# Placing the last row's receptance and first division behind a block step in a fused RWKV attention and mixture-of-experts kernel

## The chip, the core and the metric

The kernel runs on one core of a Trainium2 chip. A core has a matrix engine (PE, with its weight loads PEld), a vector engine (DVE), an activation engine (ACT), a general engine (POOL, which also issues the indirect DMAs) and SP, which here issues nearly all other DMAs. Each engine takes its instructions strictly in the order in which the program has them and waits at semaphores for the others. The metric is the device time of one execution in microseconds, the median of several runs.

## What is computed

The input x has 16 rows (batch entries) of 512 tokens of 256 channels, in float32. The reference, cut to what matters:

```
h   = layernorm(x)
xx  = h shifted by a token: channels 0-63 from before, 64-127 from behind
k, v, r = (h*mix + xx*(1-mix)) @ W.T          # three mixes, three weights
out = (a + exp(u+k)*v) / (b + exp(u+k))        # a, b: running sums over tokens
      a = a*exp(w) + exp(k)*v ; b = b*exp(w) + exp(k)
x2  = x + layernorm((sigmoid(r) * out) @ Wo.T)
t   = layernorm(x2)                            # 8192 tokens
y   = sum over the best 2 of 8 experts: gate * ((silu(t@w1.T+b1) * (t@w3.T+b3)) @ w2.T + b2)
z   = shared expert on every token, hidden width 512
result = x2 + layernorm(y + z)
```

## The kernel before

**Attention rows.** The loop over the 16 rows (L917) makes each row in steps. `front(b)` gives: sums, squares and the first norm (ACT), the turn to channels on partitions (PE transposes, L284), the mixes (DVE), the keys and values `k0` and `k1` (two halves of the channels: matmuls pk and pv at L346, exp to ek at L364 on ACT, and the two running sums at L371 on DVE), the receptance `r` (L349 to L352: four matmuls pr at L346, which the trace shows as eight pieces, and two exps to er on ACT), then per half a division `d0`, `d1` (L374 to L379: u joined to the sum, times 1 + er, and a reciprocal of 128x512, all on DVE) and a finish `f0`, `f1` (L381 to L384, giving g). `back(b)` gives the output matmuls po (L406) with their statistics, the residual and second norm, the router (L457 to L515), and eight indirect scatters of token rows into `xbuf`, a buffer in DRAM sorted by expert (L520).

**Expert blocks.** Once enough tokens of an expert lie in `xbuf`, a block of 256 of them is run. Blocks go through a pipeline, `push` (L704): one block step handles several blocks at different stages. In the order of the program it scales and scatters the oldest (`block_store`: ACT L689, POOL L691), transposes a new one (`block_turn`: px on PE L648, copied to xgT on ACT L650), makes the output of another (`block_out`: pq on PE L678, ye on DVE L682), makes the hidden layer of a third (`block_hidden`: pa and pb on PE L662, sil on ACT L665, he on DVE L667), and asks for the data of a new one (`block_load`: token rows xg at L637, weights we at L640, both on SP's queue). There are five buffers for xg, so a load of xg waits until the scatter that reads the buffer's old row numbers has landed. [...]

**The order.** For PE, DVE, ACT and SP it is written out by hand: every step of a row has a number in `ROW` (L32), with exceptions per row in `ROWS` (L33); `at(begin(b) + when[n], step)` (L889, L922) collects all steps with their times, and `in_order` (L892) issues them sorted by that number. The numbers are no times on the chip, only an order. `begin(b)` is 10 per row (L912), so row 15, the last, begins at 150. Block steps lie between the steps of the rows (L933 to L941). Around row 15's keys the order is: row 14's po1, row 15's k0 and k1 (152.61 and 152.82), row 14's residual x2 and its statistics stc (152.91 and 152.92), row 15's r (153.2) and d0 (153.51), a block step (153.9), another block step (155.9), then row 15's f0, d1 and f1 (157.4 to 157.42).

ACT evaluates exp and silu from different tables, and a table load stands in its queue where the function changes.

After the rows the rest of the blocks run back to back, then the shared expert for the remaining rows beside the loads of `ybuf` and the last norm.

Of the kernel before, what the change touches and what calls it, by code (L numbers as in the profile page):

```python
# [29 lines left out]
PERIOD = 10.0  # L30
START = [0.0, 10.0, 20.0, 30.0, 40.0]
ROW = {'x': -7.6, 'sum': -5.31, 'sq': -4.3, 'xn': -1.7, 'pt': -0.59, 'mix': 0.8, 'r': 3.2, 'k0': 2.61, 'k1': 2.82, 'd0': 3.51, 'f0': 7.4, 'd1': 7.41, 'f1': 7.42, 'po0': 9.6, 'po1': 12.6, 'x2': 12.91, 'stc': 12.92, 'xr': 17.9, 'pu': 19.21, 'pg': 19.52, 'pc': 20.43, 'sel': 21.5, 'pl': 19.22}  # L32
ROWS = {1: {'x': -8.3, 'sum': -5.6, 'sq': -4.51, 'xn': -2.5, 'pt': -1.99, 'mix': 0.0, 'r': 6.0, 'd0': 6.01, 'f1': 9.8, 'po0': 11.4, 'po1': 12.4, 'x2': 14.11, 'stc': 14.21, 'xr': 18.1, 'pu': 19.91, 'pg': 20.33, 'pc': 20.84, 'sel': 20.85, 'pl': 20.22}, 3: {'xn': -0.1, 'pt': 0.01, 'mix': 1.3, 'f0': 7.0, 'd1': 7.01, 'f1': 8.3, 'po0': 11.39, 'po1': 11.4, 'x2': 11.41, 'stc': 11.42, 'xr': 16.0, 'pu': 17.61, 'sel': 21.2, 'pl': 17.92}, 0: {'x': -7.1, 'sum': -5.11, 'sq': -1.1, 'xn': -1.09, 'pt': -1.08, 'mix': -1.07, 'r': 6.6, 'k0': -0.29, 'k1': 0.12, 'd0': 6.61, 'f0': 6.62, 'd1': 6.63, 'f1': 7.6, 'po0': 12.59, 'x2': 12.71, 'stc': 12.72, 'xr': 17.6, 'pu': 19.31, 'pg': 20.32, 'pc': 21.83, 'sel': 21.84, 'pl': 19.32}, 2: {'sq': -3.51, 'xn': -3.5, 'd0': 3.71, 'f0': 5.9, 'd1': 5.91, 'f1': 7.2, 'po0': 10.6, 'po1': 11.6, 'x2': 11.91, 'stc': 12.52, 'xr': 16.6, 'pu': 16.91, 'pc': 20.23, 'sel': 21.2, 'pl': 16.92}}  # L33
CONST_AT = 8
WHOLE_AT = -3.8
X_PARTS = 2
# [28 lines left out]
def kernel(  # L65
# [851 lines left out]
    for b in range(B):  # L917
        when = dict(ROW, **ROWS.get(b, {}))
        if b > 1:
# [178 lines left out]
```

## Time and profile before

| what | value |
|---|---|
| median of 3 runs | 1077.15 us (1076.97 to 1079.2) |
| profiled execution | 1082.54 us, span 1080.8 us |
| PE busy | 1012.6 us (94%) |
| DVE busy | 769.2 us (71%) |
| POOL busy | 569.2 us (53%) |
| ACT busy | 541.5 us (50%) |
| granted PE clock, mean | 0.979 |
| the reciprocals of the divisions (L379) | 32 of 3353 ns on DVE |
| row 15's receptance on PE | 702.26 to 705.70 us |
| row 15's first reciprocal | 711.92 to 715.27 us |

Times in the trace are microseconds from the start of the span. A row of the timeline gives the start, the duration, the engine, the line, the operation, out<-in and how many instructions were merged into it; in brackets stands how long the engine had been idle and what released it. Durations of neighbours on one engine overlap a little, so the distance between two starts tells more than a duration. Buffer numbers are left out of names. In a row of windows come the stretch, its length, the busy time and the number of instructions of PE, PEld, DVE, ACT and POOL, then the granted PE clock (1.00 is full), the DMA engines' busy share and GB/s.

### The profile page before, as it was taken

To read this page: it belongs to the slowest core of one execution; us is meant where nothing else is said; L and a number is where in the kernel's file an instruction comes from. 1 tells how busy PE (TensorE), PEld (TensorE's weight loads), DVE (VectorE), ACT (ScalarE), POOL (GpSimd) and SP (SyncE) were. 2 spreads that over 40 slices of the span, in tenths; PEclk is the share of its full clock that TensorE was granted. 3 is DMA by queue.
4 is the path that set the end of the run, shared out by engine and by line. 5 is a ranking of instruction groups with operands and counts; after the bars stand their busy time and mean duration, and the time that the engine had idled before them with its cause. 6 is when DMAs were issued, how large, how long until landed. Compare 5 with 4: busy or idle time off the path is not lost.

```text
span 1080.8 us, 15095 instructions
## 1 busy us (share of the span) xinstructions
PE 1012.6 (94%) x4202; PEld 701.4 (65%) x4202; DVE 769.2 (71%) x1905; ACT 541.5 (50%) x1150; POOL 569.2 (53%) x858
## 2 busy tenths in 40 slices
PE   5769898999999999999999999989999999999996
PEld 2335454767777677866768676667667878556554
DVE  4897696887797888878888887866353222478864
ACT  3355463657557484755757566543423333333341
POOL 2336435174656547465654646554442222369885
PEclk9789999999999999999999999989999999999998
DMA  4011313436465554645556464543556766879943
GB/s 161 6 39 38 112 71 126 151 120 192 146 200 159 175 186 154 215 153 169 154 184 189 163 192 156 171 162 119 164 196 217 246 217 207 282 246 314 314 143 114
DMA packets 80900, 181.68 MB, mean 168 GB/s; under 512 B 9597, under 2 KB 45583, under 8 KB 80816
## 3 DMA queue, kind: packets, MB, share of 16 engines
q1 hardware_dynamic: 67360, 144.89, 42.0%
q0 software_dynamic: 12736, 34.77, 8.7%
q10 hardware_dynamic: 720, 1.06, 0.3%
q8 instruction: 33, 0.54, 0.2%
q14 instruction: 51, 0.42, 0.1%
HBM read 123.12 MB, written 58.47 MB: 168 GB/s over the span
## 4 chain that ended last, share of the span: by engine, by line
PE 67%; issue 5%; ACT 4%; DVE 3%; POOL 3%; DMA 2%; SPq 0%; DVEq 0%; POOLq 0%; ACTq 0%
PE pq L678 10%; PE pa L662 9%; PE pz L749 8%; PE hs_pa L734 8%; PE pb L662 8%; PE hs_pb L734 7%; PE po L406 4%; PE pv L346 3%; PE pk L346 3%; PE pr L346 3%; PE px L648 2%; POOL xbuf L520 1%; DVE he L667 1%; PE pt L284 1%; ACT xr L278 1%
## 5 line engine op out<-in xcount | busy, mean ns | idle before, releaser
L691 POOL DMA_INDIRECT ybuf<-ye,xg x135 | 137.5, 1019 | 235.2 <-ACT ye L689 176.1
L520 POOL DMA_INDIRECT xbuf<-xr,place x128 | 134.7, 1052 | 94.3 <-DVE rest L515 46.7
L678 PE MATMUL pq<-we,he 128*128 128x256 f32 x540 | 134.2, 391 | 12.6 <-DVE he L667 11.8
L662 PE MATMUL pa<-xgT,we 128*128 128x256 f32 (+1 forms) x568 | 130.0, 372 | 0.0
L667 DVE SCALAR_TENSOR_TENSOR he<-pb,we,sil 128x256 f32<-128x256 f32 (+1 forms) x142 | 60.0, 463 | 96.7 <-PE pb L662 59.6
L662 PE MATMUL pb<-xgT,we 128*128 128x256 f32 (+1 forms) x568 | 128.3, 369 | 0.0
L734 PE MATMUL hs_pa<-xT,ws1t 128*128 128x512 f32 x256 | 120.6, 593 | 0.0
L734 PE MATMUL hs_pb<-xT,ws3t 128*128 128x512 f32 x256 | 120.3, 592 | 0.0
L678 PEld LDWEIGHTS pq<-we,he 128*128 128x128 f32 x540 | 97.6, 193 | 31.2 <-DVE he L667 17.4
L665 ACT ACTIVATE sil<-pa,we 128x256 f32<-128x256 f32 (+1 forms) x142 | 58.0, 460 | 117.7 <-PE pa L662 77.9
L749 PE MATMUL pz<-ws2t,hs 128*128 128x256 f32 x512 | 115.8, 380 | 0.2 <-DVE hs L740 0.2
L662 PEld LDWEIGHTS pa<-xgT,we 128*128 128x128 f32 x568 | 106.1, 193 | 14.2
L662 PEld LDWEIGHTS pb<-xgT,we 128*128 128x128 f32 x568 | 104.1, 190 | 13.2
L749 PEld LDWEIGHTS pz<-ws2t,hs 128*128 128x128 f32 x512 | 96.7, 190 | 19.8 <-issue 5.7
L379 DVE RECIPROCAL sb<-sb 128x512 f32<-128x512 f32 x32 | 107.3, 3353 | 1.1
L734 PEld LDWEIGHTS hs_pb<-xT,ws3t 128*128 128x128 f32 x256 | 48.6, 190 | 61.2 <-issue 56.7
L740 DVE SCALAR_TENSOR_TENSOR hs<-hs_pb,colt,hs_s 128x512 f32<-128x512 f32 x64 | 46.5, 733 | 51.9 <-PE hs_pb L734 21.7
L734 PEld LDWEIGHTS hs_pa<-xT,ws1t 128*128 128x128 f32 x256 | 48.3, 190 | 43.7 <-issue 40.1
L278 ACT ACTIVATE acc<-acc,nb_d,rs_d 128x256 f32<-128x256 f32 x64 | 34.9, 593 | 81.1 <-POOL nb_d L273 80.9
L682 DVE TENSOR_TENSOR ye<-pq,we 128x512 f32<-128x512 f32 (+1 forms) x71 | 46.7, 658 | 36.1 <-PE pq L678 31.8
L364 ACT ACTIVATE ek<-pk 128x512 f32<-128x512 f32 x32 | 18.9, 597 | 102.3 <-PE pk L346 53.7
L406 PE MATMUL po<-wa,g 128*128 128x256 f32 x256 | 63.1, 391 | 5.0 <-DVE g L384 4.9
(187 smaller groups left out, 1868.7 us busy)
## 6 DMA issues: line engine op xcount, KB each, us to landing
we<-in_we SPq DMA_DIRECT2D x71, 898.0 KB
xg<-xbuf SPq DMA_DIRECT2D x64, 258.0 KB
in<-ybuf SPq DMA_DIRECT2D x32, 512.0 KB
x<-in_x SPq DMA_DIRECT2D x15, 512.0 KB
out<-acc SPq DMA_DIRECT2D x30, 256.0 KB
x2s<-x SPq DMA_DIRECT2D x14, 512.0 KB
inx<-x2s SPq DMA_DIRECT2D x19, 256.0 KB
zs<-z SPq DMA_DIRECT2D x9, 512.0 KB
```

The lines of the kernel that those rows point to most:

```text
L346: nc.tensor.matmul(p, w[:, c, o * P : (o + 1) * P], r, start=(c == 0), stop=(c == NC - 1))
L379: nc.vector.reciprocal(sb, sb)
L406: nc.tensor.matmul(p[:, i, :], g[:, c, t * P : (t + 1) * P], woT[:, c, :], start=(c == 0), stop=(c == NC - 1))
L520: i = nc.gpsimd.indirect_dma_start(out=xbuf[:, :], out_offset=bass.IndirectOffsetOnAxis(ap=place[:, t, k : k + 1], axis=0), in_=xr[k][:, t ...
L662: nc.tensor.matmul(p[:, f, :], w[:, k : k + P], xgT[:, c, :], start=(c == 0), stop=(c == NC - 1))
L665: nc.scalar.activation(s[:, f, :], pp[0][:, f, :], AF.Silu, bias=w[:, O_B1 + f : O_B1 + f + 1])
L667: nc.vector.scalar_tensor_tensor(h[:, f, :], pp[1][:, f, :], w[:, O_B3 + f : O_B3 + f + 1], s[:, f, :], ALU.add, ALU.mult)
L678: nc.tensor.matmul(p[:, t, :], h[:, f, t * P : (t + 1) * P], w[:, k : k + C], start=(f == 0), stop=(f == NF - 1))
L682: nc.vector.tensor_tensor(y, p, w[:, None, O_B2 : O_B2 + C].to_broadcast([P, n, C]), ALU.add)
L691: j = nc.gpsimd.indirect_dma_start(out=ybuf[:, :], out_offset=bass.IndirectOffsetOnAxis(ap=xg[:, t, R_TO : R_TO + 1].bitcast(U32), axis=0) ...
L734: nc.tensor.matmul(p, w[:, c, f * P : (f + 1) * P], xT[:, c, :], start=(c == 0), stop=(c == NC - 1))
L749: nc.tensor.matmul(p[:, i, :], h[f][:, t * P : (t + 1) * P], ws2t[:, f, :], start=(f == 0), stop=(f == NS - 1))
```

## The change

Row 15 gets an entry of its own in `ROWS`, which moves its receptance from 153.2 to 155.2 and its first division from 153.51 to 155.51. Both now stand behind the block step at 153.9 and ahead of the one at 155.9. No step is added or taken out, and all other numbers stay. The diff, with the long line cut and written over several:

```diff
 ROWS = {
...
     2: {'sq': -3.51, 'xn': -3.5, 'd0': 3.71, 'f0': 5.9,
...
-}
+    15: {'r': 5.2, 'd0': 5.51}}
```

What this does to each engine's order, by the built programs:

- PE: the four pr matmuls stand behind px, pq, pa and pb of one block step instead of ahead of them.
- ACT: the two er stand behind that step's ye, xgT and sil. Before, they followed ek without a change of table; now one table load stands ahead of er and another ahead of the next sil, so ACT has two table loads more.
- DVE: L377, L378 and the reciprocal L379 of the first half stand behind that step's ye and he.
- POOL and SP: the same instructions in the same order.

More of the change, by code (lines that the diff above doesn't have):

```diff
@@ L32 @@
 ROW = {'x': -7.6, 'sum': -5.31, 'sq': -4.3, 'xn': -1.7, 'pt': -0.59, 'mix': 0.8, 'r': 3.2, 'k0': 2.61, 'k1': 2.82, 'd0': 3.51, 'f0': 7.4, 'd1': 7.41, 'f1': 7.42, 'po0': 9.6, 'po1': 12.6, 'x2': 12.91, 'stc': 12.92, 'xr': 17.9, 'pu': 19.21, 'pg': 19.52, 'pc': 20.43, 'sel': 21.5, 'pl': 19.22}
-ROWS = {1: {'x': -8.3, 'sum': -5.6, 'sq': -4.51, 'xn': -2.5, 'pt': -1.99, 'mix': 0.0, 'r': 6.0, 'd0': 6.01, 'f1': 9.8, 'po0': 11.4, 'po1': 12.4, 'x2': 14.11, 'stc': 14.21, 'xr': 18.1, 'pu': 19.91, 'pg': 20.33, 'pc': 20.84, 'sel': 20.85, 'pl': 20.22}, 3: {'xn': -0.1, 'pt': 0.01, 'mix': 1.3, 'f0': 7.0, 'd1': 7.01, 'f1': 8.3, 'po0': 11.39, 'po1': 11.4, 'x2': 11.41, 'stc': 11.42, 'xr': 16.0, 'pu': 17.61, 'sel': 21.2, 'pl': 17.92}, 0: {'x': -7.1, 'sum': -5.11, 'sq': -1.1, 'xn': -1.09, 'pt': -1.08, 'mix': -1.07, 'r': 6.6, 'k0': -0.29, 'k1': 0.12, 'd0': 6.61, 'f0': 6.62, 'd1': 6.63, 'f1': 7.6, 'po0': 12.59, 'x2': 12.71, 'stc': 12.72, 'xr': 17.6, 'pu': 19.31, 'pg': 20.32, 'pc': 21.83, 'sel': 21.84, 'pl': 19.32}, 2: {'sq': -3.51, 'xn': -3.5, 'd0': 3.71, 'f0': 5.9, 'd1': 5.91, 'f1': 7.2, 'po0': 10.6, 'po1': 11.6, 'x2': 11.91, 'stc': 12.52, 'xr': 16.6, 'pu': 16.91, 'pc': 20.23, 'sel': 21.2, 'pl': 16.92}}
+ROWS = {1: {'x': -8.3, 'sum': -5.6, 'sq': -4.51, 'xn': -2.5, 'pt': -1.99, 'mix': 0.0, 'r': 6.0, 'd0': 6.01, 'f1': 9.8, 'po0': 11.4, 'po1': 12.4, 'x2': 14.11, 'stc': 14.21, 'xr': 18.1, 'pu': 19.91, 'pg': 20.33, 'pc': 20.84, 'sel': 20.85, 'pl': 20.22}, 3: {'xn': -0.1, 'pt': 0.01, 'mix': 1.3, 'f0': 7.0, 'd1': 7.01, 'f1': 8.3, 'po0': 11.39, 'po1': 11.4, 'x2': 11.41, 'stc': 11.42, 'xr': 16.0, 'pu': 17.61, 'sel': 21.2, 'pl': 17.92}, 0: {'x': -7.1, 'sum': -5.11, 'sq': -1.1, 'xn': -1.09, 'pt': -1.08, 'mix': -1.07, 'r': 6.6, 'k0': -0.29, 'k1': 0.12, 'd0': 6.61, 'f0': 6.62, 'd1': 6.63, 'f1': 7.6, 'po0': 12.59, 'x2': 12.71, 'stc': 12.72, 'xr': 17.6, 'pu': 19.31, 'pg': 20.32, 'pc': 21.83, 'sel': 21.84, 'pl': 19.32}, 2: {'sq': -3.51, 'xn': -3.5, 'd0': 3.71, 'f0': 5.9, 'd1': 5.91, 'f1': 7.2, 'po0': 10.6, 'po1': 11.6, 'x2': 11.91, 'stc': 12.52, 'xr': 16.6, 'pu': 16.91, 'pc': 20.23, 'sel': 21.2, 'pl': 16.92}, 15: {'r': 5.2, 'd0': 5.51}}
 CONST_AT = 8
```

## The prediction

> **What bounds the kernel now.** The page first: PE is busy 94% of the span and holds 67% of the chain that ended last, so time is lost where PE stands still or runs slowly. Then the timeline of the stretch in which row 15, the last row, makes its keys and its receptance. I name blocks by the program's numbers: block 42's pq starts at 706.13, block 43's pq at 716.26, block 44's pa at 719.83, block 45's pa at 727.08, and the px at 724.46 is block 46's.
>
> ```profile
> 705.70 0.60 PE L648 MATMUL px<-ident,xg 128*128 128x128 f32 x4
> 706.13 1.89 PE L678 MATMUL pq<-we,he 128*128 128x256 f32 x8
> 707.86 1.89 PE L662 MATMUL pa<-xgT,we 128*128 128x256 f32 x8
> 709.59 1.89 PE L662 MATMUL pb<-xgT,we 128*128 128x256 f32 x8
> 711.32 0.60 PE L648 MATMUL px<-ident,xg 128*128 128x128 f32 x4
> 716.26 3.78 PE L678 MATMUL pq<-we,he 128*128 128x256 f32 x8 [4.34 <-DVE he L667]
> 719.83 3.06 PE L662 MATMUL pa<-xgT,we 128*128 128x256 f32 x8
> 722.73 1.89 PE L662 MATMUL pb<-xgT,we 128*128 128x256 f32 x8
> ```
>
> PE stands 4.34 us for block 43's he. Then pq takes 3.78 and pa 3.06 instead of 1.89: from 716.26 to 722.73 are 6.47 us for 3.46 of work (706.13 to 709.59), so 3.0 us more go to a slow clock. Why he is late stands on DVE:
>
> ```profile
> 711.92 3.35 DVE L379 RECIPROCAL sb<-sb 128x512 f32<-128x512 f32 x1
> 715.19 0.63 DVE L682 TENSOR_TENSOR ye<-pq,we 128x512 f32<-128x512 f32 x1
> 715.74 0.86 DVE L667 SCALAR_TENSOR_TENSOR he<-pb,we,sil 128x256 f32<-128x256 f32 x2
> ```
>
> Row 15's first division (L377 at 710.36, L378 at 711.19, the reciprocal) is queued ahead of ye and he, though sil (711.12 to 711.96) and pb were ready. Third view, the windows: from 735 to 782 PE is busy 47.00 of 47.00 us. What PE gains before 735 is therefore kept at least to 782; after that I find only chains that start from PE's results (router, scatters, block loads), so I carry the gain to the end.
>
> **The change, part by part.** The order of the two programs says: on PE the four pr matmuls go behind px, pq, pa, pb of one block step; on ACT the two er go behind that step's ye, xgT and sil; on DVE L377, L378 and the reciprocal go behind its ye and he. POOL and SP issue the same DMAs in the same order. ACT gets two table loads more. Nothing is taken out.
>
> PE: pr held 3.44 us (702.26 to 705.70). px 0.43, pq 1.73, pa 1.73 and pb 1.73 now start at 702.26 instead, then pr. Their inputs are there: he42 was done at 698.34, the wait for xg was over long before (load issued at 687.00), and the PSUM buffers that they and pr take over are read by 703.77 and 706.7, ahead of need. Total unchanged: block 45's px is again at 711.32. Cost 0, gain 0 up to here.
>
> ACT: x at 705.64 as before; ye at 707.45 in er's place, then by the old spacing xgT 708.24, table load 708.87, sil 710.16 to 711.00; new table load to 712.28, er 712.29 to 713.38, ye 713.25, xgT 714.04, second new load 714.67, block 44's sil 715.96 to 716.80 (its pa ends at 715.22). A load is 1.28 us on the row:
>
> ```profile
> 709.20 0.61 ACT L650 COPY xgT<-px 128x512 f32<-128x512 f32 x1
> 709.83 1.28 ACT L665 ACT_TABLE_LOAD   x1
> 711.12 0.84 ACT L665 ACTIVATE sil<-pa,we 128x256 f32<-128x256 f32 x2
> ```
>
> [...]
>
> DVE: ye at 710.36, he 710.9 to 711.8. Its first half is done before 711.5, so block 43's pq starts right behind px, at 711.75. The 4.34 us wait is gone, with the 3.0 us of slow clock behind it. Then L377 711.8; L378 waits for er to 712.9 (behind it stand the reciprocal, ye and he of block 44); reciprocal 713.6 to 717.0; ye 717.0; he 717.5 to 718.4.
>
> What is late next: PE runs pq 711.75, pa 713.48, pb 715.21 to 716.95, and wants block 46's px. Its xg load does not come earlier, for it waits for the scatters of block 41's ye, which POOL issues behind row 14's second norm:
>
> ```profile
> 710.53 0.60 POOL L268 TENSOR_SCALAR rs_c<-mv_c 128x4 f32<-128x4 f32 x1 [1.29 <-DVE mv_c L254]
> ...
> 713.89 1.09 POOL L691 DMA_INDIRECT ybuf<-ye,xg  x1 [0.62 <-issue]
> 715.29 0.97 POOL L691 DMA_INDIRECT ybuf<-ye,xg  x1 [0.30 <-issue]
> 717.98 0.31 SPq L637 DMA_DIRECT2D xg<-xbuf  x1
> ```
>
> That DVE result (710.44) stands ahead of everything that moved. The load's last landing is recorded at 720.70. So PE has a **new gap, 716.95 to 720.70: 3.75 us**, behind it pq, pa and pb. Then px 720.75, pq 721.18 (he is 2.8 us early), block 45's pa 722.91 instead of 727.08: **4.2 us earlier if the clock stays up**. The first division has slack too: from L383 at 725.50 to the last g at 733.77 were 8.27 us; from 718.4 that ends at 726.7, and PE wants g at 734.33 - 4.2 = 730.1.
>
> The clock is the other half. Windows of 3.41 us, laid on the times at which PEclk changes:
>
> ```profile
> 25.87:29.28 3.41, 1.35 (x4) 0.28 (x2) 3.27 (x4) 1.92 (x6) 2.32 (x3) 1.00 0.00 0
> 29.28:32.69 3.41, 2.49 (x8) 1.48 (x8) 3.37 (x3) 2.63 (x5) 0.29 (x3) 0.50 0.00 0
> 176.05:179.47 3.42, 1.50 (x4) 0.38 (x2) 0.47 (x2) 0.00 (x0) 2.65 (x5) 1.00 0.23 84
> 182.88:186.30 3.42, 3.42 (x5) 1.35 (x4) 2.82 (x10) 3.38 (x5) 2.04 (x4) 0.50 0.90 275
> 715.36:718.77 3.41, 2.51 (x6) 2.06 (x7) 1.24 (x3) 1.38 (x3) 2.73 (x3) 0.50 0.32 115
> 718.77:722.19 3.42, 3.42 (x9) 2.70 (x9) 0.69 (x1) 0.00 (x0) 0.12 (x1) 0.50 0.80 193
> ```
>
> First column the window, then PE's busy us; PEclk is the third number from the end. A window with 1.35 busy us is followed by half speed, one with 1.50 is not; a wholly busy window ends it, one with 2.51 doesn't. So a wait of some 2.0 us inside one window halves the clock. 3.75 us against windows of 3.41 does that for nearly every position (both parts stay under 2.0 only in 0.27 us of 3.41): one slow window costs 3.41/2 = 1.7 us, two cost the 3.0 seen now.
>
> **Sum** against the profiled execution (1082.54 us, span 1080.8): -4.2 + 1.7 = **-2.5 us** with one slow window, so 1080.0. The median of the runs is 1077.15, 5.4 below the profiled one; the stretch is the same in it, but its slow-clock share lies between 1.3 and 3.0 by the position of the windows (an estimate from the rows above). I take the same 2.5 off: **1074.6**.
>
> **Rivals.**
> - No slow window: -4.2, 1073.0. With the windows where this profile has them the gap is cut at 718.77 into 1.82 and 1.93, just under the threshold. [...] 0.20.
> - Two slow windows, as now: -4.2 + 3.0 = -1.2, 1076.0, within what counts as the same. It happens when a window ends 2.0 to 3.2 us into the gap, 1.2 of 3.41, less what the runs' own slow windows hide. 0.22.
> - The change doesn't do what it says, he43 being late by another wait (sil behind x on ACT): 1077.15. The order shows no such wait. 0.05.
> - **Slower**: block 46's xg lands later. Block 43's scatters now go out at about 719 instead of 724.44, into the stretch where this load (717.98 to 720.70) and a weight load run, the DMA engines being 0.64 busy from 717 to 722. The next weight load (issued 722.40) took 6.7 us to its last landing. At that length xg lands at 724.7, PE stands 4.0 us longer and two windows are slow: -4.2 + 4.0 + 3.0 = +2.8, 1080.0. With two slow windows it decides from 1.2 us of delay on. Against it: xg is issued ahead of those scatters. 0.13.
> - Forecast: 0.40.
>
> Range: from the case without a slow window with 1 us beyond it for the stall at 804 to 807 (PE 1.22 of 3.41 busy), which may fall in a kinder window, to the case without effect and 1 us: 1072.0 to 1078.2; only the slower case is left out. About 0.2%, 2.2 us, is what a measurement of this kernel can tell from no change. Faster: forecast and no slow window, 0.60; the same: two windows and no effect, 0.27; slower 0.13.
>
> **What would show it.** In the timeline after: px, pq, pa, pb at 702.3, pr behind pb at about 707.9; pq of block 43 at 711.8 with no wait; L379 at about 713.6; two more ACT_TABLE_LOAD rows; block 46's px at 720.7 with a wait of 3.7 us that ends with a DMA; its xg load still issued at 718.0; half speed from about 719 or 722 for one window; po of row 15 at 730 to 732 instead of 734.33. It is wrong if he43 is not done by 712, if xg is issued at another time, or if PE's lead at 735 is gone before the end.

## The result and the profile after

| | changed kernel | before |
|---|---|---|
| median of the first runs | 1076.57 us (21 runs, 1072.49 to 1078.99) | 1078.26 us (21 runs, 1076.96 to 1080.09) |
| median of later runs (beside run 9 below) | 1079.47 us (12 runs, 1077.46 to 1081.64) | 1082.84 us (26 runs, 1079.36 to 1084.99) |
| ratio, first runs | 0.998 (95%: 0.9971 to 0.9989) | |
| ratio, later runs | 0.9967 (0.9955 to 0.998) | |
| profiled execution, span | 1076.41 us, 1074.7 us | 1082.54 us, 1080.8 us |

The kernel is faster by 1.2 to 3.1 us by the first runs and by 2.2 to 4.9 us by the later ones. The two first profiles differ by more, 6.1 us, so the first question is where these lie. Here the same rows of PE stand beside each other in both profiles; he43 is short for block 43's he, and a slow window is one of the windows of 3.41 us in which the granted clock was 0.50:

| row on PE | before | after | after is later by |
|---|---|---|---|
| end of row 15's keys and values | 702.26 | 703.98 | +1.72 |
| row 15's po | 734.33 | 731.70 | -2.63 |
| hs_pa ahead of the wait near 805 | 791.61 | 788.82 | -2.79 |
| the hs_pa behind it | 813.85 | 806.93 | -6.92 |
| px at 917.59 before | 917.59 | 911.46 | -6.13 |

The stretch that the change touches, from the end of row 15's keys and values to its po, gives 4.35 us (32.07 us long before, 27.72 after). The start is 1.7 us later in this execution, long before anything that moved. Another 4.13 us come from one block's pq near 805 (told with runs 5 to 7), and 0.8 us are given back at 911. The stretch itself, after, on PE:

```profile
713.47 1.89 PE L678 MATMUL pq<-we,he 128*128 128x256 f32 x8
715.20 1.89 PE L662 MATMUL pa<-xgT,we 128*128 128x256 f32 x8
716.92 1.89 PE L662 MATMUL pb<-xgT,we 128*128 128x256 f32 x8
722.26 0.63 PE L648 MATMUL px<-ident,xg 128*128 128x128 f32 x4 [3.45 <-DMA xg<-xbuf]
722.73 1.89 PE L678 MATMUL pq<-we,he 128*128 128x256 f32 x8
724.46 1.89 PE L662 MATMUL pa<-xgT,we 128*128 128x256 f32 x8
```

Block 43's pq (first row) has no wait and no row is stretched by a slow clock. In their place stands one wait, 3.45 us for block 46's tokens, which a DMA ends. On the page the line of pq shows it too: its idle time for he is 5.9 us where it was 11.8.

```profile
L678 PE MATMUL pq<-we,he 128*128 128x256 f32 x540 | 130.9, 384 | 5.9 <-DVE he L667 5.9
```

DVE, after: block 43's he now stands ahead of the first division.

```profile
712.54 0.87 DVE L667 SCALAR_TENSOR_TENSOR he<-pb,we,sil 128x256 f32<-128x256 f32 x2
713.32 0.74 DVE L377 SCALAR_TENSOR_TENSOR sb<-ek,eu,sb 128x512 f32<-128x512 f32 x1
714.50 0.69 DVE L378 SCALAR_TENSOR_TENSOR sb<-er,sb 128x512 f32<-128x512 f32 x1 [0.43 <-ACT er L352]
715.23 3.35 DVE L379 RECIPROCAL sb<-sb 128x512 f32<-128x512 f32 x1
```

POOL and SP's queue, after: the scatters (the first two are block 41's) stand behind row 14's norm, and the load of xg behind them.

```profile
712.09 0.19 POOL L268 TENSOR_SCALAR rs_c<-mv_c 128x4 f32<-128x4 f32 x1 [1.29 <-DVE mv_c L254]
712.37 1.04 POOL L269 TENSOR_TENSOR rs_c<-rs_c,half 128x4 f32<-128x4 f32 x1
...
715.05 1.11 POOL L691 DMA_INDIRECT ybuf<-ye,xg  x1 [0.62 <-ACT er L352]
716.47 0.97 POOL L691 DMA_INDIRECT ybuf<-ye,xg  x1 [0.30 <-ACT xgT L650]
```

```profile
719.08 0.38 SPq L637 DMA_DIRECT2D xg<-xbuf  x1
```

The windows of this profile's clock grid (the 3.41 us steps at which its granted clock changes) that cut the wait, with PE's busy us first and PEclk third from the end:

```profile
716.87:720.28 3.41, 1.94 (x9) 1.36 (x8) 3.41 (x5) 2.39 (x5) 2.50 (x3) 1.00 0.33 102
720.28:723.69 3.41, 1.43 (x9) 1.35 (x10) 3.31 (x5) 0.59 (x1) 2.89 (x6) 1.00 0.90 204
```

Both keep more than 1.35 busy us, and the clock stays at 1.00 from 187.8 us to the tail of the kernel. The grid cuts the wait into two parts, 1.47 and 1.98 us of idle time in their windows. In the first profile of before it was otherwise: the window ahead of the two slow ones had no work of PE at all.

```profile
711.95:715.36 3.41, 0.00 (x0) 0.00 (x0) 3.41 (x2) 0.01 (x1) 2.40 (x5) 1.00 0.00 0
```

### The profile page after: what moved, and what is told of

It is laid out like the page before. It is cut to its first block, busy times and chain, and to the rows that moved or that the text cites. A ratio compares the mean times of both kernels' runs of the same rounds, so it can differ in the third digit from the quotient of the medians.

```text
span 1074.7 us, 15097 instructions
## 1 busy us (share of the span) xinstructions
PE 1009.1 (94%) x4202; PEld 699.9 (65%) x4202; DVE 767.5 (71%) x1905; ACT 544.3 (51%) x1152; POOL 570.3 (53%) x858
## 4 chain that ended last, share of the span: by engine, by line
PE 56%; DVE 9%; ACT 6%; DMA 5%; POOL 5%; issue 4%; SPq 0%; DVEq 0%; ACTq 0%; POOLq 0%
PE pq L678 8%; PE pz L749 8%; PE pa L662 7%; PE hs_pb L734 7%; PE hs_pa L734 7%; PE pb L662 7%; PE po L406 3%; PE pv L346 2%; PE pk L346 2%; DMA x<-in_x 2%; POOL xbuf L520 2%; PE pr L346 2%; DVE he L667 2%; DMA xg<-xbuf 1%; PE px L648 1%
## 5 line engine op out<-in xcount | busy, mean ns | idle before, releaser
L678 PE MATMUL pq<-we,he 128*128 128x256 f32 x540 | 130.9, 384 | 5.9 <-DVE he L667 5.9
L379 DVE RECIPROCAL sb<-sb 128x512 f32<-128x512 f32 x32 | 107.3, 3353 | 1.1
L278 ACT ACTIVATE x<-po,nb_b,rs_b 128x256 f32<-128x256 f32 x64 | 30.9, 563 | 72.5 <-DVE sa L371 33.2
```

The costliest lines, as they stand in the source:

```text
L278: nc.scalar.activation(dst, src, AF.Identity, bias=nb[:, t : t + 1], scale=rs[:, t : t + 1])
L379: nc.vector.reciprocal(sb, sb)
L678: nc.tensor.matmul(p[:, t, :], h[:, f, t * P : (t + 1) * P], w[:, k : k + C], start=(f == 0), stop=(f == NF - 1))
```

## The experiments

Theory: he43 was late because the division stood ahead of it on DVE. With that gone, block 46's tokens set when PE goes on, and they hang on POOL's order and on the number of buffers, not on what was moved. The slow clock decides the size of the gain. Rivals: the receptance's move matters (as cover for the wait, or by its two table loads); what PE gains is lost again later; the gain comes from the place near 805.

Runs 1 to 4, 5 to 8 and 9 to 12 are three sets, each on a chip of its own with before beside it. Before's medians were 1078.05, 1080.93 and 1082.84 us, so I compare ratios across sets.

**1. The division alone.** Edit of the changed kernel:

```diff
-    15: {'r': 5.2, 'd0': 5.51}
+    15: {'d0': 5.51}
```

> Only the division is moved (d0 at 155.51); the receptance stays at 153.2, so ACT has no table load more. Theory: the gain comes from the division leaving DVE's queue ahead of block 43's he, and then block 46's token load sets when PE goes on, whatever lies ahead of it. pq of block 43 then waits at most 0.6 us, block 46's px starts 18.3 us behind the end of row 15's keys and values (722.26 - 703.98 in the changed kernel), within 0.5, and the time is that of the changed kernel within 1 us, 0.7 to 2.7 below before. Rival 1: the receptance is needed behind the block step to cover the wait for he; pq then waits 2 us or more and the time is within 0.7 us of before. Rival 2: the two added table loads cost something in the changed kernel; this one is then over 1 us below it.

1074.74 us against 1078.05, ratio 0.9963 (0.9949 to 0.9977). On PE:

```profile
712.33 1.99 PE L678 MATMUL pq<-we,he 128*128 128x256 f32 x8 [0.25 <-DVE he L667]
...
720.30 0.63 PE L648 MATMUL px<-ident,xg 128*128 128x128 f32 x4 [2.53 <-DMA xg<-xbuf]
```

Block 43's pq waits 0.25 us, and block 46's px starts 17.87 us behind the keys (702.43 to 720.30; 18.28 in the changed kernel), both within what the theory gave. So the receptance isn't needed as cover. The time came out 3.3 us below before, a little more than the 0.7 to 2.7 expected; run 12 asks whether the table loads have a part in that.

**2. Work in the new wait.** The first of the shared expert's last steps goes ahead of block 46's px:

```diff
-        at(begin(B - 1) + ROW["po0"] + (i + 0.5) * (ROW["sel"] - ROW["po0"]) / LAST_BESIDE, shared_step)
+        at(begin(B - 1) + 6.5 if i == 0 else begin(B - 1) + ROW["po0"] + (i + 0.5) * (ROW["sel"] - ROW["po0"]) / LAST_BESIDE, shared_step)
```

> The changed kernel with the first of the shared expert's last steps (sixteen pz matmuls on PE, 3.46 us by their rows) moved from 160.6 to 156.5, ahead of block 46's px. Theory: the wait of 3.45 us for block 46's tokens is real time of PE and the lead is kept to the end; with work in it the wait at that px is under 0.6 us, no half speed starts in this stage, and the time falls by 3.0 to 5.5 us below the changed kernel (3.4 for the wait, up to 2 for the slow clock that follows it in some runs). Rival: what PE gains here is lost again at later waits; then the time is within 1 us of the changed kernel although the wait is gone.

1072.02 us, ratio 0.9945 (0.9932 to 0.9958):

```profile
718.27 3.62 PE L749 MATMUL pz<-ws2t,hs 128*128 128x256 f32 x16
722.31 0.66 PE L648 MATMUL px<-ident,xg 128*128 128x128 f32 x4 [0.43 <-DMA xg<-xbuf]
```

Of the wait 0.43 us is left. By the ratios this is 0.22% (later runs of the changed kernel) to 0.35% (first runs) below the changed kernel, 2.4 to 3.8 us, where 3.0 us left the wait. The ratios come from different chips, and the interval overlaps a little with that of the later runs (0.9955 to 0.998). On the same chip run 1's kernel, with a like wait of 2.53 us, had 1074.74 us, 2.7 above this one. So most of what left the wait reaches the end, and that speaks against a later loss.

**3. Six buffers for xg, after the change.**

```diff
-        xg = wp.tile([P, 2, R_END], F32, tag="xg", name=f"xg{q}", bufs=4 + LEAD)[:, 0:n]
+        xg = wp.tile([P, 2, R_END], F32, tag="xg", name=f"xg{q}", bufs=5 + LEAD)[:, 0:n]
```

> The changed kernel with six buffers for xg instead of five; same instructions in the same order. Theory: block 46's load waits for the scatters of block 41, which read the buffer that it takes over; with one buffer more it waits for block 40's, long landed, and is issued over 4 us earlier than 719.08; the wait of 3.45 us at block 46's px is under 0.5 and the time is 3.0 to 5.5 us below the changed kernel. Rival: the load is held by the queue of SP or by the weights' buffers, is issued within 1 us of now, and the time stays within 1 us.

1070.06 us, ratio 0.9932 (0.9919 to 0.9945), the fastest of set 1 and 4.7 us below run 1. Block 46's load goes out 4.0 us behind the keys' end (701.31 here) instead of 15.1 (719.08 - 703.98):

```profile
705.34 0.38 SPq L637 DMA_DIRECT2D xg<-xbuf  x1
```

```profile
715.98 0.60 PE L648 MATMUL px<-ident,xg 128*128 128x128 f32 x4
716.90 1.99 PE L678 MATMUL pq<-we,he 128*128 128x256 f32 x8 [0.32 <-DVE he L667]
```

The px has no wait, the next pq 0.32 us. This shows the chain from block 41's scatter over the buffer and the load to px: with another buffer the wait is gone.

**4. Row 14's norm behind the block step.** Edit of the changed kernel: `14: {'stc': 14.0}` added to `ROWS`.

> The changed kernel with row 14's second-norm statistics (stc) moved from 152.92 to 154.0, behind the block step at 153.9. Theory: block 41's scatters stand on POOL behind that norm; ahead of it they go out 3 us earlier, block 46's load is asked for at about 716 instead of 719.08, the wait at its px falls from 3.45 to under 1 us, and the time is 2.0 to 4.5 us below the changed kernel. Rival: the norm is then late for row 14's pu, whose rows already wait 0.16 us for xr; a wait of 2 us or more appears there and the time stays within 1.5 us of the changed kernel.

1072.75 us, ratio 0.9955 (0.9942 to 0.9968). POOL, SP's queue, then PE:

```profile
709.02 1.09 POOL L691 DMA_INDIRECT ybuf<-ye,xg  x1 [0.18 <-issue]
710.42 0.98 POOL L691 DMA_INDIRECT ybuf<-ye,xg  x1 [0.30 <-ACT sil L665]
```

```profile
713.06 0.38 SPq L637 DMA_DIRECT2D xg<-xbuf  x1
```

```profile
716.70 0.60 PE L648 MATMUL px<-ident,xg 128*128 128x128 f32 x4
719.10 1.99 PE L678 MATMUL pq<-we,he 128*128 128x256 f32 x8 [1.80 <-DVE he L667]
```

Counted from the keys' end (702.03 here) scatters and load are 4.1 us earlier than in the changed kernel (load 11.0 instead of 15.1), a little more than the 3 expected, and the wait for tokens is gone. The rival's wait (pu for xr) doesn't appear. Another does: the next block's he (718.57) stands behind the moved reciprocal (714.76 to 718.11), the mechanism of before one block later and 1.80 us long. Row 14's statistics (L253 and L254, 711.07 to 713.28) now stand on DVE between the block step's he and that division, so counted from the keys' end the reciprocal starts 1.5 us later than in the changed kernel; there the wait for tokens covers he's lateness, and in run 3 only 0.32 us of it was left.

**5 to 7. Second and third profiles of both kernels** (no edit).

> The kernel before once more, for a second profile. Theory: its first profile (1082.54 us, 4.4 above the median of its runs) holds a stall of 4.1 us at 804 to 812 that most runs do not have; it is missing here and the time lies between 1077 and 1080. The wait for block 43's he is again 4.3 us, within 0.3, and behind it lie one or two windows of half speed. Rival: the stall belongs to the kernel before, is here again, and the change took it away; the gain of the profiles is then due to that place as much as to the moved division.

> The changed kernel once more, for a second profile. Theory: its runs lie further apart (1072.5 to 1079.0) than those of before (1077.0 to 1080.1) because the wait for block 46's tokens lies at the edge at which the clock halves; the wait is 2.5 to 4 us again, and here, unlike in the first profile, one window or two of half speed may begin between 716 and 724, with 1.7 to 3.4 us more from the end of row 15's keys and values to po than the 27.7 of the first profile (731.70 - 703.98). Rival: this stretch is 27.7 us, within 0.7, whatever the run's time, and the runs differ elsewhere.

> The same kernel a third time, as before: the stretch from the end of row 15's keys and values to po is 27.7 us without a window of half speed, 29 to 31 with one or two (theory), or 27.7 within 0.7 whatever the run's time (rival).

Times 1078.79, 1075.83 and 1077.0 us, before's median beside them 1080.93. Before, again:

```profile
715.69 3.59 PE L678 MATMUL pq<-we,he 128*128 128x256 f32 x8 [3.63 <-DVE he L667]
...
804.78 1.99 PE L678 MATMUL pq<-we,he 128*128 128x256 f32 x8 [2.07 <-DVE he L667]
```

The wait for he43 is 3.63 us, shorter than I gave it, with one slow window (715.55 to 718.96) in place of two. The second row refutes my theory of the place near 805: the wait of about 2.1 us is in this profile too. But the rival falls as well, for the changed kernel has it in its second and third profile (2.05 and 2.06 us). All eight profiles of sets 2 and 3 have it, whichever kernel, and none of the four of set 1, which are all of kernels with the division moved. Something else in the traces goes with it. Before's first profile and these eight hold 10,444 to 10,687 semaphore counts of the engines; the first profile of the changed kernel and those of set 1 hold 13,388 to 13,392. So the wait goes with where or how a profile was taken, and no pair of profiles shows that the change took it away. I therefore don't count it as gain that before's first profile had it, with a slow window behind it (4.13 us), and after's lacked it. Whether the timed runs have this wait is not shown.

The stretch of the changed kernel was 27.09 and 27.59 us, the wait 2.82 and 3.30 us, no window slow. Here the rival is right: the stretch hardly varies.

**8. Six buffers without the change.**

> The kernel before with six buffers for xg instead of five. Theory: before, block 46's tokens are not what PE waits for; he43 behind the reciprocal is. The wait of 4.3 us for he43 stays, with its slow clock, and the time is 0 to 2 us below before (the wait of 1.0 us at 917 may go). The sixth buffer is worth 5 us or more only after the change (1070.1 against 1076.6 there). Rival: the sixth buffer is worth its 6 us everywhere, by loads that come earlier throughout; then this kernel is 5 us or more below before.

1080.78 us against 1080.93, ratio 0.9996 (0.9977 to 1.0014): nothing that can be measured. The wait for he43 stands as before, and the rows behind it are slow:

```profile
716.85 3.78 PE L678 MATMUL pq<-we,he 128*128 128x256 f32 x8 [4.20 <-DVE he L667]
720.42 3.15 PE L662 MATMUL pa<-xgT,we 128*128 128x256 f32 x8
```

The sixth buffer is worth 0.35 to 0.48% after the change (0.9932 against 0.9967 and 0.998) and nothing measurable ahead of it. In kernels with the division alone it is 0.32% (0.9931 of run 12 against 0.9963 of run 1).

**9. The changed kernel, timed again, with a fourth profile** (no edit).

> The changed kernel itself, timed beside the next three. Theory: 1.5 to 4.5 us below before, 27 to 28 us from the end of row 15's keys and values to po where no window is slow, and up to 3.4 more where one or two are. Rival: it is within 1 us of before on this chip, and the gain of 1.7 to 2.2 us measured at first was chance.

1079.47 us against 1082.84, ratio 0.9967. The stretch is 27.10 us, the wait 2.73. But in this profile a slow window begins 0.3 us ahead of row 15's po:

```profile
725.78:729.19 3.41, 2.39 (x25) 1.12 (x23) 1.32 (x3) 2.44 (x6) 1.03 (x1) 1.00 0.78 242
729.19:732.61 3.42, 3.37 (x9) 2.74 (x10) 2.40 (x18) 1.39 (x3) 0.00 (x0) 0.50 0.58 215
```

```profile
729.51 3.42 PE L406 MATMUL po<-wa,g 128*128 128x256 f32 x8
```

The po takes 3.42 us instead of 1.90. Counted from the keys' end, this execution is 4.97 us ahead of before's first profile at the start of po and only 2.79 ahead at the hs_pa ahead of the wait near 805. The slow window took 1.5 us of that, and a wait of 0.54 us for he at 761, which before's first profile lacks, most of the rest. So in this profile part of the gain of the stretch is lost a few us behind it.

**10 and 11. Idle matmuls inside each wait.** Nothing reads them; they only keep PE busy. In the changed kernel six of them ahead of block 46's px, in before seven ahead of block 43's pq:

```diff
+    def warm(n): [nc.tensor.matmul(p, ident, ws2t[:, 0, :], start=True, stop=True) for p in ([bank([P, C], "warm")] if n else []) for _ in range(n)]
...
-        q, xg, n = i["q"], i["xg"], i["n"]
+        q, xg, n = i["q"], i["xg"], i["n"]; warm(6 if q == 46 else 0)
```

> The changed kernel with six idle matmuls (ident by ws2t, twelve pieces of 0.22 us, 2.6 us; nothing reads them) ahead of block 46's px, inside the wait for its tokens. PE then has too little idle time there for a slow window, and no work is saved. Theory: in the changed kernel's runs the wait is often followed by a slow window; this one is then 0.7 to 2 us below the changed kernel. Rival (all three profiles so far had no slow window there): the clock costs nothing there, and the times agree within 0.6 us.

> The kernel before with seven idle matmuls (3.0 us; nothing reads them) ahead of block 43's pq, inside the wait for he. The wait for he stays as long, only the slow clock behind it goes. Theory: one or two windows are slow there in every profile of before, worth 1.2 to 3.0 us; this kernel is 1.2 to 3.0 us below before, and the wait alone (4.3 us) remains. Rival: the clock costs under 0.7 us in most runs; then this one is within 0.7 us of before, and the change should have gained the whole of its 4.2 us less what the wait for tokens costs.

Changed kernel with them: 1080.69 us, ratio 0.9989 (0.9975 to 1.0003), against 0.9967 without. That is 1.2 us above the changed kernel, with intervals that overlap: not the gain of the theory, nor the 0.6 us of the rival. In the profile the tokens came late: px starts 19.16 us behind the keys' end, against 17.56 to 18.28 in the four profiles of the changed kernel, so that 1.65 us of wait followed the idle work. If the timed runs are like that, the lateness could hide a small gain; that no clock is lost in that wait rests on the four profiles.

```profile
715.81 2.75 PE L632 MATMUL warm<-ws2t,ident 128*128 128x256 f32 x12
720.22 0.66 PE L648 MATMUL px<-ident,xg 128*128 128x128 f32 x4 [1.65 <-DMA xg<-xbuf]
```

Before with them: 1078.16 us against 1082.84, ratio 0.9962 (0.9947 to 0.9976), 2.6 to 5.7 us faster though PE gets he43 no earlier (pq starts 14.22 us behind the keys' end, 14.00 in before's first profile):

```profile
712.50 3.19 PE L632 MATMUL warm<-ws2t,ident 128*128 128x256 f32 x14
717.23 1.99 PE L678 MATMUL pq<-we,he 128*128 128x256 f32 x8 [1.54 <-DVE he L667]
```

```profile
712.77:716.18 3.41, 2.92 (x14) 2.23 (x12) 3.38 (x3) 0.17 (x1) 2.48 (x4) 1.00 0.00 0
716.18:719.60 3.42, 2.37 (x11) 2.08 (x12) 1.73 (x5) 1.38 (x3) 2.66 (x3) 1.00 0.32 115
```

No window is slow here, and the pq takes 1.99 us instead of 3.78. I expected 1.2 to 3.0 us; the interval begins at 2.6, and what goes beyond the clock of this stretch is not explained. The median granted clock of all runs rose from 0.980 to 0.984. This edit, which shortens no wait, was worth as much on this chip as the whole change (0.9962 and 0.9967). The changed kernel's runs there had 0.984 as well, and its stretch is 2.3 us shorter in the profiles (27.10 against 29.37); that these 2.3 us of time reach the end does not show in the runs of this chip.

**12. The division alone, with six buffers.** Edits of runs 1 and 3 together.

> Only the division moved (receptance back at 153.2, no table load more) and six buffers for xg. With the wait for block 46's tokens gone, what the receptance's move and its two table loads cost or gain can be seen. Theory: nothing; the time is that of the changed kernel with six buffers (1070.06; 8.0 below before) within 0.8 us. Rival: the table loads cost; it is 1 us or more below that. Second rival: the receptance behind the block step covers the wait for he; it is 1 us or more above.

1075.06 us against 1082.84, ratio 0.9931 (0.991 to 0.9952). Run 3, with the receptance moved as well, had 0.9932. So the receptance's new place and its two table loads cost and gain nothing that can be measured; with these intervals, on two chips, an effect below 2 to 3 us would not be seen. By the profiles the stretch is 0.4 us shorter with the receptance moved (24.67 against 25.08). On ACT of the changed kernel they stand like this:

```profile
712.57 1.28 ACT L352 ACT_TABLE_LOAD   x1
713.87 1.09 ACT L352 ACTIVATE er<-pr 128x512 f32<-128x512 f32 x2
...
716.24 1.28 ACT L665 ACT_TABLE_LOAD   x1
717.53 0.84 ACT L665 ACTIVATE sil<-pa,we 128x256 f32<-128x256 f32 x2
```

Each load takes 1.28 us, and each activation starts 0.02 us or less behind its load.

All profiles of the stretch together:

| kernel | waits of PE in it, us | keys' end to row 15's po, us | slow windows ahead of po |
|---|---|---|---|
| before | he 4.34 | 32.07 | 2 |
| before, again | he 3.63 | 30.03 | 1 |
| before, six buffers | he 4.20 | 32.01 | 2 |
| before, idle matmuls | idle work 3.0, he 1.54 | 29.37 | 0 |
| changed | tokens 3.45 | 27.72 | 0 |
| changed, again, third, fourth | tokens 2.82, 3.30, 2.73 | 27.09, 27.59, 27.10 | 0 (the fourth: one 0.3 us ahead) |
| division alone | he 0.25, tokens 2.53 | 27.31 | 0 |
| changed, shared step in the wait | tokens 0.43 | 28.17, with 3.5 of other work in it | 0 |
| changed, idle matmuls | idle work 2.6, tokens 1.65 | 28.62 | 0 |
| changed, norm later | he 1.80 | 26.14 | 0 |
| changed, six buffers | he 0.32 | 24.67 | 0 |
| division alone, six buffers | he 0.25 and 0.21 | 25.08 | 0 |

## Why the prediction came out as it did

**What bound it: right.** With the division out of he43's way alone (run 1) the wait is 0.25 us.

**PE's order: right.** Four blocks of matmuls and pr changed places at no cost: block 45's px stands at 713.03, less the 1.72 us of the start 711.31, predicted 711.32.

**ACT's table loads: right.** Predicted er at 712.29 and sil at 715.96; after, 713.87 and 717.53, less 1.72, 712.15 and 715.81. Run 12 finds no cost that can be measured.

**The new wait: right in place and cause, a little too long.** I took 3.75 us from the landing in before's trace; measured were 3.45, 2.82, 3.30 and 2.73. The step that erred is that nothing that moved reaches POOL's chain. No instruction of it moved, but its durations did: the norm's L268 and L269 took 0.60 and 1.56 us before, and 0.19 and 1.04 us after.

```profile
710.53 0.60 POOL L268 TENSOR_SCALAR rs_c<-mv_c 128x4 f32<-128x4 f32 x1 [1.29 <-DVE mv_c L254]
711.22 1.56 POOL L269 TENSOR_TENSOR rs_c<-rs_c,half 128x4 f32<-128x4 f32 x1
```

What ran beside them on DVE before were the first two steps of the division, L377 (710.36 to 711.08) and L378 (711.19 to 711.88); after, both steps come later (L271, beside L377 then, took 0.76 us instead of 0.22). The long reciprocal is not the cause: before's L269 of an earlier row, wholly beside a reciprocal (104.06 to 107.41), took 1.04 us.

```profile
105.85 1.04 POOL L269 TENSOR_TENSOR rs_a<-rs_a,half 128x4 f32<-128x4 f32 x1
```

The load goes out 0.6 us earlier (719.08 less 1.72 is 717.36, predicted 717.98), of which the norm gives 0.4 and an earlier start of L268 0.2. Between profiles of one kernel the load moves as much: 15.72 and 14.96 us behind the keys' end before, 14.66 to 15.26 after.

**The 4.2 us with the clock up: right.** Row 15's po came 4.35 us nearer to the keys' end. Of this 2.7 us is clock and 1.65 is time: with the clock held up, before needs 29.37 us (run 11) and the first profile of after 27.72. In before's second profile, with one slow window, the clock's part is only 0.66 us (30.03 less 29.37).

**The 1.7 us of one slow window: wrong as to place.** I gave 0.40 to one slow window in the new wait and 0.20 to none. Four profiles of four have none, and keeping PE busy there gains nothing that shows (run 10). The threshold that I read from before's rows (half speed behind 1.35 busy us, none behind 1.50) was my estimate; the shorter wait and the cut by the grid left this wait's windows above 1.35, the idlest one shown with 1.43 busy us, and the clock stayed at 1.00. Other windows do not fit it (last section). This is the rival without a slow window. The sum took nearly every position of the grid to be bad. In the first and the fourth profile the grid cuts the wait 1.63 and 1.87 us after its start; with 2.0 us as the limit and all positions alike, waits of 2.73 to 3.45 us would escape in 16 to 37% of them (an estimate from these figures). Whether four of four was luck, or the position is not free, stays open. What took the window's place in the sum differs by run: one window 0.3 us ahead of po in the fourth profile, a wait of 1.78 us at 911 instead of 0.99 in the first.

**The sum.** Predicted -2.5 us. Measured -1.7 (-1.2 to -3.1) and -3.4 (-2.2 to -4.9): the size is right, but the term of +1.7 in it is not what the profiles show, so that the number came out is in part luck. By the profiles the stretch should give 3.7 us (31.05, the mean of before's two, less 27.38, the mean of after's four). Where the first runs lose 2 us of that isn't settled: 21 runs stand against one profile, and the places that vary (windows at the start, the wait near 805, a wait for he at 761) vary in both kernels.

**The lead to the end: right but for 0.8 us.** From 735 to 900 only the place near 805 changes the distance between the two first profiles by more than 0.2 us; in run 9's profile the wait at 761 does too. At the px of 911 tokens are late again, by 0.8 us more than before.

**The slower rival** did not come: the load landed 3.2 us behind its issue, 2.7 before, in spite of the scatters beside it (719.01 and 720.28).

## What to carry to other kernels

The matrix engine's wait for he43 had two prices here, the time (4.34 us in before's first profile) and the slow clock behind it (granted 0.50 in two windows there); idle matmuls in the wait separated them, and the clock was about half of what the change gained in the profiles (1.7 us, 31.05 less 29.37, of 3.7). Before a late instruction is freed, look for what the same engine wants next: here a buffer held the next tokens, so that everything ahead of them could be put in another order for nothing, and a sixth buffer, which gave nothing before, then gave at least about as much again as the change itself. And an engine whose order was untouched still kept another pace where other instructions ran beside it on its neighbour: POOL's L269 took 1.56 us with L378 on DVE beside its start, and 1.04 after the change.

## What the runs showed of the hardware

- The norm's pow on POOL (L269, row 14) took 1.56 or 1.57 us in the profiles in which L378 of a division ran on DVE beside its start (before, run 4, run 5, run 8, run 11) and 1.04 in the four profiles of the changed kernel and in runs 1, 2, 3 and 10. L268 took 0.59 or 0.60 us beside L377 and 0.19 or 0.20 without. Wholly beside a reciprocal L269 took 1.04 us and L268 0.19 (before, 105.57 to 106.89).
- A window with 2.39 of 3.41 us busy, its rows mostly transposes and very small matmuls, was followed by half speed (run 9: po 3.42 us). Behind the same rows po took 1.90 us in runs 5 and 6, and windows with 1.94 and 1.43 busy us were not followed by half speed (the first profile of the changed kernel, 716.87 and 720.28). Busy time alone doesn't decide there. In before's first profile half speed also followed a window with 0.00 busy us (711.95 to 715.36) and windows that were not idle, with 1.35 (25.87 to 29.28) and 1.22 (804.11 to 807.52). At the start of that profile two windows with 0.00 (1.98 to 8.80) were not followed by it: the clock stayed at 1.00 until 29.28.
- Near 805 the wait of 2.0 to 2.2 us for he comes from a sil that starts long after its pa. In the second profile of the changed kernel ACT shows it:

```profile
800.77 0.84 ACT L665 ACTIVATE sil<-pa,we 128x256 f32<-128x256 f32 x2 [8.88 <-issue]
```

Its pa is recorded as done by 794.2. In before's first profile, where this sil starts at 805.84 and its pa is done by 799.10, five of PE's semaphore counts stand together, from 805.76 to 806.03, and the one ahead of them at 800.01. It came on two chips in all eight profiles and in before's first profile, and on the chip of runs 1 to 4 in none. The traces with it hold a fifth fewer semaphore counts than the others (10,646 in before's first profile, 13,389 in the changed kernel's), and some of PE's counts there are not recorded. What holds the counts back stays open.
